# Graph attention and a DiT block on one core: self features of six more tiles added by VectorE, and two boundaries and the end in another order

## The chip, the cores and the metric

The kernel runs on one core of one Trainium2 chip. Its engines work side by side, each through its own queue in order: TensorE (PE; its weight loads are shown as PEld), VectorE (DVE), ScalarE (ACT), GpSimd (POOL), and SyncE (SP), which here only issues DMAs. The metric is the device time of one execution in microseconds, the median of several runs. An engine that waits for another waits on a semaphore, and whatever stands behind the waiting instruction in the same queue waits too.

## What is computed

Input x is 64 sequences of 64 tokens of 256 features. First a graph attention with a residual, then a transformer block whose norms are modulated by a condition:

```python
# graph attention, two directions d, 16 heads, 20 keys per sequence
self_feat = concat(v, q) @ W_self.T + b_self
output = self_feat
for d in range(2):
    aff = einsum('bnhd,bmhd->bnhm', qh, kh) / sqrt(dh)
    aff = where(cond > 0, aff, NEG) + (A_d @ w_bias + b_bias)
    out_t = einsum('bnhm,bmf->bnhf', softmax(aff), kv)
    output = output + einsum('bnhf,hgf->bnhg', out_t, Wout) + bout
x = v + relu(output)
# block: shift, scale, gate from silu(cond) @ Wt + bt
h = layernorm(x) * (1 + scale_msa) + shift_msa
x = x + gate_msa * (attention(h) @ Wproj + bproj)
h = layernorm(x) * (1 + scale_mlp) + shift_mlp
x = x + gate_mlp * (gelu(h @ W1 + b1) @ W2 + b2)
```

All of it is float32.

## The kernel before, in words

The 64 sequences are cut into nine groups of 4, 8, 8, 8, 8, 8, 8, 8 and 4 (numbers 0 to 8); two sequences make a tile of 128 tokens, so a group has 4 tiles, the outer ones 2. Features lie on partitions (`xT`, `sfT`, `hT`: 128 partitions, 2 halves c, tokens). The residual stream of a group stays in `xT`, is added to in place, and is stored from there.

The order is written out by hand: each function records its instructions on the engines it uses, and the order of the calls is the order in every queue. `start` does group 0's graph part, `boundary(g)` stands between the periods, `period(g)` runs the tiles of a group, `finish` ends. A `slot` takes one tile e of block attention and one tile c of the next group's graph attention: scores of both (L755, L756), then the softmax parts, with the transposes, attention products and outputs of the slot before (Eb, Cb), and other work put in by name (`fill("f1")` and so on). While group g is in block attention, group g+1 is in graph attention, g−1 in its MLP, and g+2 has its self features and masks made. The parts that matter:

- `graph_turned` (L490): eight transposes of the weights to PSUM (pwT), two ScalarE copies to wT. `graph_output` (L502): 16 small products of wT with `vblk` into po. For groups 0 to 2 (`early`, L507) two products with the identity first put self features into po, and ScalarE takes the relu straight from PSUM (L521). For the others VectorE adds po to sf (L523) and ScalarE takes the relu in SBUF (L524). POOL adds the result to xT (L525).
- `norm_tokens` (L528): four transposes of xT (pxT), a ScalarE copy xn; `norm_stats` (L537): five VectorE instructions and a power on POOL (L546); `normed` (L548): two VectorE instructions (L551); `modulated` (L556): four transposes (phT), a VectorE product (L563), a POOL sum (L567).
- `graph_exp` (L476): VectorE maxima and subtraction, ScalarE exp. `graph_normal` (L483): sum, reciprocal, POOL product (L488). `block_exp`, `block_sums`, `block_weights` (L624 to L643): the same for block attention, with a POOL product pr (L643).
- `mask_step(g, i)` (L338): seven VectorE steps for a group's masks and biases, 0 to 2 for one direction, 3 to 5 for the other, 6 for three last instructions.
- `graph_v` (L363): values, through DRAM (L374, L389) into vblk (L395). `graph_q` (L416): one of four q products (pqT), copied by ScalarE.
- `block_qk` (L573), `block_keys` (POOL, L597), `block_attended` (L659: pao, copied by ScalarE at L675). `block_proj` (L686): the projection of a whole group for one half c. `pair_proj` (L697): the same for two tiles and both halves.
- `mlp_up`, `mlp_down` (L717, L727), `mlp_gated`, `mlp_out` (L735, L743): the last ends with the store of a half.

PSUM has eight banks. Scores use two pairs ("pa", "pb"); `bank` (L89) hands out the other four in turn, and an accumulator of `mlp_down` holds its bank until `mlp_gated`:

```python
    def bank(name, hold=False):
        tag = free.pop(0)
        if not hold:
            free.append(tag)
        t = ps.tile([P, 512], F32, tag=tag, name=name)
        return (t, tag) if hold else t
```

A bank's new user waits for the last reader of its old contents.

In `boundary(g)` VectorE's order around the graph output is: values, mask steps (from 2 on at g = 1, all seven at g = 2, steps 4 to 6 later), then what follows graph_output.

Of the kernel before, what the change touches and what calls it, by code (L numbers as in the profile page):

```python
# [9 lines left out]
F32 = mybir.dt.float32  # L10
# [7 lines left out]
P = 128  # L18
# [28 lines left out]
def graph_attention_then_dit_block(  # L47
# [454 lines left out]
    def graph_output(t, po):  # L502
# [3 lines left out]
        po2 = po[:, 0:D].rearrange("p (c t) -> p c t", c=2)  # L506
        early = t.g < 3  # L507
        if early:
# [187 lines left out]

    def pair_proj(g, j2):  # L697

        G = groups[g]
        py = bank("pproj").rearrange("p (c t) -> p c t", c=2)  # L700
        t2 = ts(j2, 2 * P)
        for c in range(2):
            for k in range(2):
                nc.tensor.matmul(
                    py[:, c], wproj_sb[:, k, ts(c, P)], G.aoT[:, k, t2], start=(k == 0), stop=(k == 1)
                )
        y = two.tile([P, GT], F32, tag="tq", name="y").rearrange("p (c t) -> p c t", c=2)
# [6 lines left out]
        nc.gpsimd.tensor_tensor(G.xT[:, :, t2], G.xT[:, :, t2], y, ALU.add)  # L714

# [35 lines left out]
    def slot(e, c, e_next, c_next, before, fill, late=False):  # L751
# [29 lines left out]
        fill("d0b")  # L781
        if E:

            block_weights(E)
# [3 lines left out]
        for i, t in enumerate(Cb):  # L788
# [3 lines left out]
            graph_output(t, pair("pa" if i > 0 else "pb", "po")[:, 0])  # L792
        if C and late:
            graph_exp(C)
        fill("f2b")
        fill("d1")
# [6 lines left out]
    def boundary(g, before):  # L803
# [8 lines left out]
        if c_on:  # L812
            graph_v(g + 1, 1)
            for i in range((2, 0)[g - 1] if g < 3 else 4, 7):
                mask_step(g + 1, i)
        if m_on and c_on:
            mlp_out(g - 2, 1)
        block_turned(Eb)
        for t in Cb:
            graph_turned(t)  # L820
        if not c_on:
            mlp_down(g - 2, 1, *range(4))
        if c_on:
# [11 lines left out]
        if Cb:  # L835
            norm_tokens(G, G.xT, 1)
            norm_stats(G)
        block_proj(g - 1, 0)
        if Cb:
            normed(G)  # L840
        block_proj(g - 1, 1)
        if c_on:
            graph_q(g + 1, 1, 0)
        if Cb:
            modulated(G, G.hT, 1, amp1, off1, g)
        K = [Tile() for _ in range(A.nt // 2)]
        if not c_on:
            mlp_down(g - 2, 1, 4, 5)
        if c_on:
            graph_k(g + 1, 1)  # L850
        for j2, k in enumerate(K):
            norm_tokens(k, A.xT, j2)
            norm_stats(k)
# [16 lines left out]
        if e_on:  # L870
            block_qk(g, 0, 1)
        if c_on:
            graph_q(g + 1, 1, 1)
# [31 lines left out]
    def period(g):  # L905
# [35 lines left out]
        else:  # L941
# [38 lines left out]
    def start():  # L980
# [74 lines left out]
        for t in t1:  # L1055
# [27 lines left out]
                "f2a": [(self_product, 2, 1)],  # L1083
                "f3": [
                    (self_features, 2, 1), (mask_step, 2, 0), (block_v, 0, 0), (half_normed, 1, 0),
                    (mask_step, 2, 1), (time_projection, 3),
                ],
            },
# [4 lines left out]
                "f2b": [(time_product, 4), (time_product, 5), (time_sum, 4), (time_sum, 5)],  # L1093
                "f3": [(half_normed, 1, 3), (time_added, 4)],
            },
# [3 lines left out]
    def finish(before):  # L1099
# [83 lines left out]
        mlp_out(z, 0)  # L1183
        mlp_down(z, 1, *range(8))
        mlp_gated(z, 1)
        mlp_out(z, 1)

# [64 lines left out]
```

## Time and profile before

| what | value |
|---|---|
| median of 3 runs | 685.67 us (683.94 to 686.73) |
| profiled execution | 682.96 us |
| its span in the profile | 681.3 us |
| granted TensorE clock | 1.0 |
| idle before PE matmuls: start, 0 to 12 us | 2.3 us |
| 12 to 60 | 2.3 us |
| stretch 60 to 105 (end of start, boundary 1) | 4.5 us |
| 105 to 147 (period 1) | 2.0 us |
| 147 to 543, five periods with their boundaries | about 0.4 us |
| 543 to 578 (boundary 7) | 1.1 us |
| 604 to 653 (finish) | 2.9 us |
| 673 to 681.3 (end) | 4.2 us |

The profile is one execution on the hardware, and its times are in microseconds unless they are marked ns. A float32 matmul shows as two records, so counts of PE rows are twice the number of matmuls in the code. A timeline row has the start, the time, the engine, the line, the operation, the output and the inputs, the shapes and the count; in brackets stands how long the engine had been idle and what ended that. Rows of PE overlap, since matmuls are pipelined: the distance from one start to the next is what a row costs, not its length. A wait row has who waited, for whom, the total, how often, and the longest.

### The profile page before, as it was taken

What the parts mean: (1) busy time and instruction counts of PE and PEld (TensorE: products, weight loads), DVE (VectorE), ACT (ScalarE), POOL (GpSimd) and SP (SyncE); (2) the same over time, 40 slices, a digit from 0 to 9 for tenths busy, and PEclk for the clock granted to TensorE, in tenths of its full rate; (3) what the DMA queues carried; (4) which work ended last, traced back from release to release, by engine and by line L of the source; (5) the groups of instructions that cost most, each with busy time, mean ns of one, the idle gap of its engine ahead of it and who ended that gap; (6) DMA issues with size and microseconds to landing.
All of it is one profiled execution on the core that took longest, in us unless ns stands there. A gap on an engine that the chain in (4) does not pass through costs nothing.

```text
span 681.3 us, 15434 instructions
## 1 busy us (share of the span) xinstructions
PE 661.0 (97%) x6422; PEld 405.4 (60%) x6422; DVE 477.6 (70%) x849; ACT 354.6 (52%) x627; POOL 375.4 (55%) x371
## 2 busy tenths in 40 slices
PE   8999899999999999999999999999999999999997
PEld 7656657775555555556556555555565655556456
DVE  4988956797787677875876867776777865666221
ACT  3355437653576437654476435764377446754412
POOL 6555455755584476645584656744666456355220
PEclk9999999999999999999999999999999999999999
DMA  9535040004000220004000141002000000000000
GB/s 280 163 89 166 21 134 17 18 21 135 17 1 29 70 90 16 7 27 154 1 17 17 36 135 17 2 32 72 27 10 11 17 26 1 3 16 1 17 15 32
DMA packets 34382, 33.42 MB, mean 49 GB/s; under 512 B 5608, under 2 KB 28200, under 8 KB 34312
## 3 DMA queue, kind: packets, MB, share of 16 engines
q1 hardware_dynamic: 33352, 31.74, 15.1%
q8 instruction: 51, 0.84, 0.5%
q0 software_dynamic: 272, 0.33, 0.3%
q10 hardware_dynamic: 688, 0.35, 0.2%
q14 instruction: 19, 0.16, 0.1%
HBM read 25.59 MB, written 6.83 MB: 48 GB/s over the span
## 4 chain that ended last, share of the span: by engine, by line
PE 78%; DVE 13%; ACT 3%; POOL 2%; issue 2%; DMA 1%; SPq 0%; ACTq 0%; POOLq 0%; DVEq 0%
PE pu L723 14%; PE py L733 13%; PE pqT L422 8%; PE pqk L580 7%; PE ppT L654 4%; PE pv L588 3%; PE pf L324 3%; PE pwT L496 3%; PE pproj L690 3%; PE po L514 2%; PE pv L371 2%; PE pk L407 2%; PE phT L560 2%; PE pao L665 2%; PE sca L618 2%
## 5 line engine op out<-in xcount | busy, mean ns | idle before, releaser
L733 PE MATMUL py<-u,w 128*128 128x512 f32 (+1 forms) x288 | 121.4, 551 | 0.2 <-ACT u L725 0.2
L723 PE MATMUL pu<-h2T,w 128*128 128x512 f32 (+1 forms) x256 | 108.8, 570 | 0.5 <-POOL h2T L567 0.5
L643 POOL TENSOR_TENSOR pr<-pr,sm 128x1024 f32<-128x1024 f32 x32 | 60.8, 1901 | 66.9 <-DVE sm L642 64.0
L474 POOL TENSOR_TENSOR w<-w,term 128x640 f32<-128x640 f32 x32 | 49.4, 1547 | 77.8 <-DVE w L469 40.3
L723 PEld LDWEIGHTS pu<-h2T,w 128*128 128x128 f32 x256 | 47.9, 190 | 48.6 <-issue 42.7
L733 PEld LDWEIGHTS py<-u,w 128*128 128x128 f32 x288 | 50.8, 190 | 36.4 <-issue 33.0
L725 ACT ACTIVATE u<-pu,vec 128x512 f32<-128x512 f32 (+1 forms) x72 | 43.3, 639 | 35.5 <-PE pu L723 35.2
L422 PE MATMUL pqT<-sfT,wq 128*128 128x512 f32 (+1 forms) x144 | 60.9, 551 | 0.7 <-DVE a L350 0.7
L580 PE MATMUL pqk<-hT,wqkv 128*128 128x512 f32 (+1 forms) x144 | 59.7, 552 | 0.6 <-POOL hT L567 0.4
L629 DVE TENSOR_REDUCE mx<-sca 128x8 f32<-128x512 f32 x32 | 22.1, 691 | 51.8 <-PE sca L458 50.3
L551 DVE TENSOR_SCALAR xn<-xn,mv,rstd 128x256 f32<-128x256 f32 x64 | 50.1, 823 | 7.7 <-POOL rstd L546 7.7
L639 DVE TENSOR_REDUCE sm<-pr 128x16 f32<-128x1024 f32 x32 | 38.9, 1217 | 21.4 <-ACT pr L635 20.7
L481 ACT ACTIVATE w<-w 128x640 f32<-128x640 f32 x32 | 23.6, 736 | 54.4 <-DVE w L480 54.4
L542 DVE BATCH_NORM_STATS2 st<-xn 128x6 f32<-128x256 f32 x64 | 26.1, 408 | 34.7 <-ACT xn L535 34.7
L488 POOL TENSOR_TENSOR w<-w,sm 128x640 f32<-128x640 f32 x32 | 44.0, 1376 | 11.7 <-DVE sm L487 11.5
L423 ACT ACTIVATE qT<-pqT,vec 128x512 f32<-128x512 f32 (+1 forms) x36 | 23.0, 639 | 52.6 <-PE pqT L422 52.5
L635 ACT ACTIVATE pr<-pr 128x1024 f32<-128x1024 f32 x32 | 33.8, 1057 | 30.1 <-DVE pr L631 29.9
L546 POOL TENSOR_TENSOR rstd<-rstd,mhalf 128x2 f32<-128x2 f32 x32 | 23.3, 728 | 46.7 <-DVE rstd L545 45.9
L657 ACT COPY pT<-ppT 128x512 f32<-128x512 f32 x64 | 34.4, 590 | 26.4 <-PE ppT L654 26.4
L581 ACT ACTIVATE qk<-pqk,vec 128x512 f32<-128x512 f32 (+1 forms) x36 | 23.0, 640 | 43.3 <-PE pqk L580 43.3
L500 ACT COPY wT<-pwT 80x512 f32<-80x512 f32 x64 | 34.0, 581 | 13.9 <-PE pwT L496 13.9
L525 POOL TENSOR_TENSOR xT<-xT,sfT 128x256 f32<-128x256 f32 x32 | 24.1, 753 | 28.6 <-ACT sfT L524 16.3
(144 smaller groups left out, 1424.6 us busy)
## 6 DMA issues: line engine op xcount, KB each, us to landing
xT<-in_x_t SPq DMA_DIRECT2D x7, 512.0 KB
out<-xT SPq DMA_DIRECT2D x14, 256.0 KB
a_d<-in_adj SPq DMA_DIRECT2D x7, 440.0 KB
a_d<-in_adj_t SPq DMA_DIRECT2D x7, 440.0 KB
x_g<-in_x SPq DMA_DIRECT2D x5, 512.0 KB
vblk<-vd SPq DMA_DIRECT2D x28, 80.0 KB
w<-in_w SPq DMA_DIRECT2D x2, 1024.0 KB
vd<-v_sb SPq DMA_DIRECT2D x7, 256.0 KB
```

The source lines that it names most:

```text
L422: nc.tensor.matmul(pq, wq_sb[d][:, k, ts(c, P)], G.sfT[:, k, :], start=(k == 0), stop=(k == 1))
L474: nc.gpsimd.tensor_tensor(t.w, t.w, G.term[:, :, j, :].unsqueeze(1).to_broadcast([P, H, 2, M]), ALU.add)
L488: nc.gpsimd.tensor_tensor(wf, wf, sm.unsqueeze(2).to_broadcast([P, 2 * H, M]), ALU.mult)
L500: nc.scalar.copy(t.wT[:, ts(q4, 4), :], pt[0 : 4 * M, :].rearrange("p (i t) -> p i t", i=4))
L551: nc.vector.tensor_scalar(key.xn[:, i, :], key.xn[:, i, :], key.mv[:, i, 0:1], key.rstd[:, i : i + 1], ALU.subtract, ALU.mult,)
L580: nc.tensor.matmul(pp, wqkv_sb[:, k, ds(i * D + c * P, P)], G.hT[:, k, 0 : G.T], start=(k == 0), stop=(k == 1))
L639: nc.vector.tensor_reduce(t.sm, t.pr, AX.X, ALU.add)
L643: nc.gpsimd.tensor_tensor(t.pr, t.pr, t.sm.unsqueeze(2).to_broadcast([P, H, N]), ALU.mult)
L657: nc.scalar.copy(t.pT[:, ts(q4, 4), :], pt.rearrange("p (i t) -> p i t", i=4))
L723: nc.tensor.matmul(pu, w1_sb[:, k, ts(m, P)], G.h2T[:, k, 0 : G.T], start=(k == 0), stop=(k == 1))
L725: nc.scalar.activation(G.u[m], pu, AF.Gelu, bias=col("b1", m))
L733: nc.tensor.matmul(G.py, w2_sb[:, m, ts(c, P)], G.u[m], start=(m == 0), stop=(m == 7))
```

## The change

It has seven edits.

1. `early` holds for group 0 and the first two tiles of group 1 only, so for tiles (1,2), (1,3) and (2,0) to (2,3) the two identity products go, and VectorE adds self features.
2. In a slot marked late, `block_weights` is recorded after the graph output and `graph_exp`. In the first slot of the start, `self_features(2, 1)` comes at d1, and mask step 1 of group 2 leaves for boundary 1.
3. In boundary 1 the mask steps are 3, 1, 2, 4 ahead of the transposes and 5, 6 behind the graph output, followed by `time_added(4)`, which was in the start. `graph_q(2, 0, 0)` moves ahead of the second transposes, and `graph_q(2, 1, 1)` from the end of the boundary to behind `graph_q(2, 1, 0)`.
4. In the periods, the third step of `half_normed` (`normed`) is recorded at d0b, ahead of `block_weights`, and no longer at d1.
5. Boundary 7 has an order of its own, with the projection by pairs of tiles, the two q products earlier and the second pair's transposes between qk products.
6. In period 7 a down product moves behind attention. In the finish one pao takes a bank of the four instead of a pair; v and the scores of z's second tile come behind two down products and a norm; a down product comes ahead of the last transposes but one.
7. The last half of the last group is computed, gated, added and stored in two parts of 128 tokens.

```diff
-        early = t.g < 3
+        early = t.g == 0 or (t.g == 1 and j < 2)
...
-        if E:
+        if E and not late:
             block_weights(E)
...
-        if C and late:
+        if late:
             graph_exp(C)
+            block_weights(E)
...
-            for i in range((2, 0)[g - 1] if g < 3 else 4, 7):
+            for i in (3, 1, 2, 4) if g == 1 else range(0 if g == 2 else 4, 7):
                 mask_step(g + 1, i)
...
         block_turned(Eb)
+        if g == 1:
+            graph_q(2, 0, 0)
         for t in Cb:
             graph_turned(t)
...
+        if g == 1:
+            mask_step(2, 5)
+            mask_step(2, 6)
+            time_added(4)
...
+        if g == NG - 2:
+            pair_proj(g - 1, 0)
             norm_tokens(G, G.xT, 1)
             norm_stats(G)
             normed(G)
+            pair_product(g - 1, 1)
             graph_q(g + 1, 1, 0)
+            norm_tokens(K[0], A.xT, 0)
+            pair_gated(g - 1, 1)
             modulated(G, G.hT, 1, amp1, off1, g)
+            pair_added(g - 1, 1)
+            graph_q(g + 1, 1, 1)
+            graph_k(g + 1, 1)
+            norm_stats(K[0])
...
             block_qk(g, 1, 0)
+            if g == NG - 2:
+                norm_tokens(K[1], A.xT, 1)
+                norm_stats(K[1])
             block_qk(g, 1, 1)
...
-        if c_on:
+        if c_on and g not in (1, NG - 2):
             graph_q(g + 1, 1, 1)
...
-                    "d1": next_(half_normed, 2),
+                    "d0b": next_(half_normed, 2),
...
+            fills[1].update(f0=down(0, 0), f2=down(0, 1))
...
-        block_attended(before[0], pair("pa", "pao")[:, 0])
+        block_attended(before[0], bank("pao"))
...
-        block_v(z, 0)
         block_normal(E0)
-        E1 = block_scores(z, 1, [pair("pa", "sca"), pair("pb", "scb")])
-        mlp_down(l, 1, 4)
+        mlp_down(l, 1, 4, 5)
         norm_tokens(K[1], A.xT, 1)
         norm_stats(K[1])
-        mlp_down(l, 1, 5, 6)
+        block_v(z, 0)
+        E1 = block_scores(z, 1, [pair("pa", "sca"), pair("pb", "scb")])
         normed(K[1])
         block_turned(E0)
+        mlp_down(l, 1, 6)
...
+        mlp_down(m, 0, 0)
         block_turned(E1)
-        mlp_down(m, 0, 0)
...
-        mlp_down(z, 1, *range(8))
-        mlp_gated(z, 1)
-        mlp_out(z, 1)
+        py, y = bank("py"), two.tile([P, GT], F32, tag="tq", name="y")
+        for j in range(2):
+            t = ts(j, P)
+            for i in range(8):
+                nc.tensor.matmul(py[:, t], w2_sb[:, i, P : 2 * P], Z.u[i][:, t], start=(i == 0), stop=(i == 7))
+            nc.vector.scalar_tensor_tensor(
+                y[:, t].rearrange("p (b n) -> p b n", n=N), py[:, t].rearrange("p (b n) -> p b n", n=N), col("b2", 1),
+                gate[:, 3, ds(Z.b0 + 2 * j, 2)].unsqueeze(2).to_broadcast([P, 2, N]), ALU.add, ALU.mult,
+            )
+            nc.vector.tensor_tensor(Z.xT[:, 1, t], Z.xT[:, 1, t], y[:, t], ALU.add)
+            nc.sync.dma_start(out[P : 2 * P, ds(Z.t0 + j * P, P)], Z.xT[:, 1, t])
```

`pair_product`, `pair_gated` and `pair_added` are `pair_proj` cut in three: its products, its two VectorE instructions, and POOL's add.

More of the change, by code (lines that the diff above doesn't have):

```diff
@@ L695, in block_proj, with pair_product @@
         nc.gpsimd.tensor_tensor(G.xT[:, c, :], G.xT[:, c, :], G.yT[c], ALU.add)
-    def pair_proj(g, j2):
+    def pair_product(g, j2):
         G = groups[g]
-        py = bank("pproj").rearrange("p (c t) -> p c t", c=2)
-        t2 = ts(j2, 2 * P)
+        py = G.pair = bank("pproj").rearrange("p (c t) -> p c t", c=2)
         for c in range(2):
@@ L704, in pair_proj, with pair_gated @@
                 nc.tensor.matmul(
-                    py[:, c], wproj_sb[:, k, ts(c, P)], G.aoT[:, k, t2], start=(k == 0), stop=(k == 1)
+                    py[:, c], wproj_sb[:, k, ts(c, P)], G.aoT[:, k, ts(j2, 2 * P)], start=(k == 0), stop=(k == 1)
                 )
-        y = two.tile([P, GT], F32, tag="tq", name="y").rearrange("p (c t) -> p c t", c=2)
+    def pair_gated(g, j2):
+        G = groups[g]
+        py = G.pair
+        y = G.yp = two.tile([P, GT], F32, tag="tq", name="y").rearrange("p (c t) -> p c t", c=2)
         b4 = ds(G.b0 + 4 * j2, 4)
@@ L713, in pair_proj, with pair_added @@
             )
-        nc.gpsimd.tensor_tensor(G.xT[:, :, t2], G.xT[:, :, t2], y, ALU.add)
+    def pair_added(g, j2):
+        G = groups[g]
+        t2 = ts(j2, 2 * P)
+        nc.gpsimd.tensor_tensor(G.xT[:, :, t2], G.xT[:, :, t2], G.yp, ALU.add)
+    def pair_proj(g, j2):
+        pair_product(g, j2)
+        pair_gated(g, j2)
+        pair_added(g, j2)
     def mlp_up(g, m):
@@ L822, in boundary @@
             mlp_down(g - 2, 1, *range(4))
-        if c_on:
+        if c_on and g > 1:
             graph_q(g + 1, 0, 0)
@@ L834, in boundary @@
             load_adj(g + 2)
-        if Cb:
+        K = [Tile() for _ in range(A.nt // 2)]
+        if g == NG - 2:
+            pair_proj(g - 1, 0)
             norm_tokens(G, G.xT, 1)
             norm_stats(G)
-        block_proj(g - 1, 0)
-        if Cb:
             normed(G)
-        block_proj(g - 1, 1)
-        if c_on:
+            pair_product(g - 1, 1)
             graph_q(g + 1, 1, 0)
-        if Cb:
+            norm_tokens(K[0], A.xT, 0)
+            pair_gated(g - 1, 1)
             modulated(G, G.hT, 1, amp1, off1, g)
[L846 to L849, printed above, removed]
+            pair_added(g - 1, 1)
+            graph_q(g + 1, 1, 1)
             graph_k(g + 1, 1)
-        for j2, k in enumerate(K):
-            norm_tokens(k, A.xT, j2)
-            norm_stats(k)
+            norm_stats(K[0])
+        else:
+            if Cb:
+                norm_tokens(G, G.xT, 1)
+                norm_stats(G)
+            block_proj(g - 1, 0)
+            if Cb:
+                normed(G)
+            block_proj(g - 1, 1)
+            if c_on:
+                graph_q(g + 1, 1, 0)
+            if g == 1:
+                graph_q(2, 1, 1)
+            if Cb:
+                modulated(G, G.hT, 1, amp1, off1, g)
+            if not c_on:
+                mlp_down(g - 2, 1, 4, 5)
+            if c_on:
+                graph_k(g + 1, 1)
+            for j2, k in enumerate(K):
+                norm_tokens(k, A.xT, j2)
+                norm_stats(k)
         if c_on:
@@ L871, in boundary @@
             block_qk(g, 0, 1)
-        if c_on:
+        if c_on and g not in (1, NG - 2):
             graph_q(g + 1, 1, 1)
@@ L1083, in start @@
                 "f2a": [(self_product, 2, 1)],
[L1084 to L1087, printed above, removed]
+                "d1": [(self_features, 2, 1)],
+                "f3": [(mask_step, 2, 0), (block_v, 0, 0), (half_normed, 1, 0), (time_projection, 3)],
             },
@@ L1093, in start @@
                 "f2b": [(time_product, 4), (time_product, 5), (time_sum, 4), (time_sum, 5)],
-                "f3": [(half_normed, 1, 3), (time_added, 4)],
+                "f3": [(half_normed, 1, 3)],
             },
```

## The prediction, made before the run

> **What bounds the kernel now.** I read the page first, then the windows by stage, the PE waits, and the timelines of the stages that the change touches.
>
> ```profile
> PE 661.0 (97%) x6422; PEld 405.4 (60%) x6422; DVE 477.6 (70%) x849; ACT 354.6 (52%) x627; POOL 375.4 (55%) x371
> ```
> TensorE is busy for 661.0 of 681.3 us at a granted clock of 1.0. Only two things shorten this kernel: less TensorE work, or less of its 20 us of idle time. Where the idle time sits:
>
> ```profile
> 60.00:105.00 45.00, 40.47 (x465) 27.03 (x463) 33.49 (x62) 18.72 (x37) 21.90 (x24) 1.00 0.19 60
> 227.33:306.67 79.34, 79.28 (x775) 45.53 (x774) 59.01 (x104) 43.53 (x74) 47.18 (x45) 1.00 0.15 44
> ```
> Columns: stretch, length, then PE, PEld, DVE, ACT and POOL busy. A period of the middle has 0.06 us of idle PE, so no order can help there. The stretch with boundary 1 has 4.5 us, 105 to 147 has 2.0, 543 to 578 has 1.1 and 604 to 653 has 2.9. By cause (total, times, longest):
>
> ```profile
> PE phT L560 <- DVE xn L551: 2.6, 4, 1.5
> PE pao L665 <- DVE w L469: 1.8, 1, 1.8
> PE pwT L496 <- POOL w L488: 1.3, 2, 0.8
> PE pwT L496 <- DVE v_sb L387: 0.8, 1, 0.8
> PE pao L665 <- DVE pr L631: 0.7, 1, 0.7
> ```
> These are what the reordering can reach. The matmuls that it removes:
>
> ```profile
> 118.84 0.65 PE L665 MATMUL pao<-pT,v 128*32 128x64 f32 x32
> 119.42 0.71 PE L510 MATMUL po<-sfT,ident 128*128 128x128 f32 x4
> 120.06 0.74 PE L514 MATMUL po<-wT,vblk 80*32 80x64 f32 x32
> 120.73 1.98 PE L324 MATMUL pf<-xT,w_self 128*128 128x512 f32 x4
> ...
> 192.62 0.65 PE L665 MATMUL pao<-pT,v 128*32 128x64 f32 x32
> 193.10 0.80 PE L514 MATMUL po<-wT,vblk 80*32 80x64 f32 x32
> 193.83 1.99 PE L324 MATMUL pf<-xT,w_self 128*128 128x512 f32 x4
> ```
> From attention to the next product it is 1.89 us with the identity products and 1.21 without: 0.68 us a tile. Next to v's product (129.93 to 132.96 against 206.43 to 209.01) it is 0.45.
>
> **The change, part by part.** All sums are against the profiled execution.
>
> *Six adds to VectorE.* PE loses three times 0.65 and three times about 0.5: 3.4 us. VectorE gains six adds of 0.39 us (row of L523, 22 calls, 0.36 to 0.43): 2.4 us, with ScalarE's relu now behind them.
>
> *Start, 58 to 75.* VectorE takes the softmax subtraction before the reciprocal; it ran for 2.02 us beside POOL's 1.90 us product and should take its usual 0.83. One mask step (1.08) leaves. VectorE is then free when the scores end (65.4), so the maxima start at 65.5 rather than 66.32 and attention's wait falls from 1.75 to about 0.95: 0.8 gained. POOL now adds both tiles before its product, which waits for the second relu (61.6) and ends at about 64.3; the transposes that need it come at 65.6, so 1.3 us cover it. At 73.9 phT still meets VectorE, so this tile's identity saving is not seen yet.
>
> *Boundary 1, 75 to 104.* v_sb now stands ahead of amp/off (0.37 + 1.35 + 1.01), and a q product (1.72) comes ahead of the second transposes: the waits 0.52 and 0.76 vanish, and 0.64 of identity goes. At the end of L514 PE is 3.3 us ahead (81.2 for 84.5). The new add stands behind four mask steps (4.3 us from 77.5): 81.9 to 82.3, then relu 0.4 and POOL's add 0.75 give pxT at 83.65 where PE is there at 82.9: a new wait of 0.75. Stats are behind two more mask steps and amp/off, but two q products cover them (phT 89.25, before 90.83). The later waits for hT and xn (0.15 and 0.6) stay about as they are. The last q product no longer hides ScalarE's copy of the last qk (0.69): half of the scores wait 0.45. Graph scores at 101.0 instead of 104.37: 3.3 us gained in all, identity included.
>
> *Period 1, 105 to 147.* Slots 1 and 2 give 0.68 and 0.45; VectorE has 0.8 and 1.26 us to spare there, which its adds use up. In the last slot xn (2.27 us beside POOL) moves ahead of the reciprocal and takes 0.73; phT ends its wait 1.5 us earlier, but POOL's products start 0.7 later on that chain and w reaches pwT late: about 1.0 of it is left.
>
> *Boundary 2.* Here the add hurts.
> ```profile
> 148.91 0.29 DVE L387 TENSOR_TENSOR v_sb<-pv,bout 128x128 f32<-128x128 f32 x1 [0.72 <-PE pv L382]
> 149.12 1.06 DVE L347 TENSOR_REDUCE cnt<-a_d 128x80 f32<-128x880 int32 x1
> ...
> 156.05 0.38 DVE L360 SCALAR_TENSOR_TENSOR term<-vb,bb,term 128x160 f32<-128x160 f32 x1
> ```
> VectorE's queue holds the seven mask steps without a gap, 7.3 us, and the add for tile 3 is recorded behind them. Before, ScalarE did the relu straight from PSUM at 154.43 and pxT ran at 156.11 unhindered. On the new clock v_sb is at 146.35, the masks end at 153.95, add, relu and POOL's add take 1.6: pxT at 155.6, while PE would be there at 153.2. 2.4 us of new idle time, with proj, q and everything of PE queued behind it. The lead at this pxT: 156.1 − 155.6 = 0.5 on top of 3.3, so 3.8.
>
> *Periods 2 to 6.* normed moves ahead of the reciprocal. PE has no wait there to lose; the reciprocal comes 0.7 later, and POOL's product would end at about 305.05 for a transpose at 308.26. Nothing, covered by 3 us.
>
> *Boundary 7.* Projection by pairs costs PE the same (1.73 + 1.73 for 3.44). It removes pxT's waits (0.5 each), but brings four: phT on xn (0.7), qk on hT (0.55), phT of the first pair, whose normed now stands on VectorE behind the second pair's stats, which need POOL's 1.27 us add, a transpose and a copy (1.0 to 1.5), and the uncovered last copy (0.4). Graph scores at 567.9 for 566.95: 0.95 lost; between 0.5 gained and 1.8 lost.
>
> *Period 7.* One down product goes behind attention; the wait 0.45 at 584.23 is set by ScalarE (copy, table load 1.28, exp 1.06, then wT), so it stays: nothing.
>
> *Finish.* pao moves from the pair to a bank and the 0.70 wait goes. But the bank is the one that the next held accumulator takes, and its reader stands late on ScalarE:
> ```profile
> 608.23 1.06 ACT L635 ACTIVATE pr<-pr 128x1024 f32<-128x1024 f32 x1
> 609.19 0.61 ACT L675 ACTIVATE aoT<-pao,vec 128x128 f32<-128x128 f32 x2
> ```
> PE idles from 606.9 to 609.85, and scores E0 come 1.0 late. The two down products put behind the projection, and v later, absorb that: at 630 it is 0.2 late. The down product ahead of the last transposes covers their 0.61: 0.6 gained net.
>
> *Last store.* Sixteen 256-column matmuls become thirty-two of 128. [...] The trace disagrees: eight transposes with 128x128 loads follow each other every 0.116 us (187.29 to 188.22), 256-column ones every 0.215, so 3.71 for 3.44: 0.27 lost. I take the trace. After PE, gate and add over 128 columns: 0.48 + 0.42 become about 0.35 + 0.29 (from the 512- and 256-column rows): 0.26 gained. The store: 3.0 us from issue (678.26) to the span's end; no row has 64 KB to HBM. [...] Sum: 0.2 gained, between 0.2 and 0.4; by the loads rule 1.3 lost.
>
> Sum: 3.8 − 0.95 + 0 + 0.6 + 0.2 = 3.65 us. The profiled execution took 682.96 (span 681.3 and 1.66 around it): 679.3. The runs' median is 685.67, 2.7 above; I take the same difference: **682.0**.
>
> **The rivals.** *All covers hold*: VectorE finishes the masks before boundary 2's po, or pairs cost nothing at boundary 7. Then 2.4 of the new wait and 0.95 come back: 3.65 + 2.0 + 0.95 = 6.6, 679.1. For it: the middle's boundaries have this very chain without a wait (312.35 to 314.79), with three mask steps. Against: boundary 2 has all seven.
> *The waits only change place*: PE loses 3.4 of work and each edit's gain meets the next late engine, above all in boundary 1, where VectorE has no gap of 1 us between 77 and 89. Then 3.4 less 2.4 (boundary 2), less 0.95, plus half of the rest (1.3): 1.3 gained, 684.4. This is also the case in which the order does not do what it is meant to.
> *Slower: VectorE's queue is the bound from 64 to 160.* Place: boundary 1's add and the stats behind it. If amp/off run at their contended 1.35 and 1.01, and the mask steps at 1.1 push stats past 89, phT waits to 93 and boundary 1's 3.3 turns into 0.5 lost; the slots give nothing, boundary 2's pxT is 2.0 late, boundary 7 loses 0.95, the finish and the store give 0.8: 2.6 lost, 688.3. It decides from an add of tile (1,3) that starts after about 84 on the old clock, against my 81.9. Against it: amp/off leave POOL's busy stretch (77.5 to 80).
>
> **How the numbers follow.** Forecast 0.42, all covers 0.27, waits change place 0.23, slower 0.08. 0.5% (3.4 us) is about what a measurement of this kernel tells from no change. The forecast lies just past it, some 0.6 of its cases beyond: faster 0.27 + 0.25 = 0.52, same 0.17 + 0.23 = 0.40, slower 0.08. Range: from the all-covers case with the end's best (678.7) to the misplaced waits with boundary 7's worst (685.2).
>
> **What would show it.** In the profile after: L510 x16 instead of x40 and PE busy near 658; L523 x28; no pwT wait on v_sb; a pxT wait on POOL's L525 of about 2.4 us near 153 (right: my boundary 2; absent: the first rival) and one below 1 us near 83 (larger: the slower case); a phT wait on xn above 1 us near 560; a py wait on aoT or its bank near 607; the last 32 matmuls in 3.7 us. If phT still waits 1.5 us at the end of period 1, the order of normed was not the cause. The prediction is wrong if boundary 1 gains under 2 us.

## The result, and the profile after

The changed kernel takes 684.39 us (median of 14 runs, 681.49 to 687.03), the kernel before 684.5 (median of 14 runs, 683.39 to 686.73). The ratio is 0.9993 with a 95% interval of 0.9976 to 1.001: no change. The forecast was 682.0 with a range from 678.7 to 685.2, so the time lies in the range, near its upper end, and the likeliest class, faster, did not come. The forecast had started from 685.67, a median of three runs; fourteen give 684.5.

The profiled execution took 687.03 us (span 685.3, granted clock 0.993), the slowest run of this kernel, and the profile of before had 682.96 (681.3, 1.0). Its page has for TensorE and the rest:

```profile
PE 662.1 (97%) x6422; PEld 407.6 (59%) x6422; DVE 468.2 (68%) x859; ACT 354.6 (52%) x627; POOL 371.8 (54%) x371
```

TensorE's busy time has risen by 1.1 us though products for 3.4 us are gone, because in two places the same products ran at half the clock (0.50, in the windows below). VectorE has more instructions and less busy time. To see where time went I use the start of every first product that writes graph scores into `scb` as an anchor: there are 30 in each trace, at the same places of the program. All values are us; the forecast column is the sum of the prediction's own steps.

| stretch, by anchors of before | before | after | difference | forecast |
|---|---|---|---|---|
| 0 to 65.24: start | 65.24 | 69.13 | +3.89 | 0 |
| 65.24 to 104.70: its end, boundary 1 | 39.46 | 36.51 | −2.95 | −3.3 |
| 104.70 to 135.83: three slots of period 1 | 31.13 | 32.22 | +1.09 | −0.5 with the next |
| 135.83 to 175.05: last slot, boundary 2 | 39.22 | 39.28 | +0.06 | see above |
| 175.05 to 492.40: periods 2 to 6 | 317.35 | 316.34 | −1.01 | 0 |
| 492.40 to 567.27: boundary 7 | 74.87 | 75.81 | +0.94 | +0.95 |
| 567.27 to the end: period 7, finish, store | 114.03 | 116.01 | +1.98 | −0.8 |
| span | 681.3 | 685.3 | +4.0 | −3.65 |

The first row is not the change's: no instruction ahead of 57 us has moved. The list of TensorE's waits (total, times, longest) begins so:

```profile
PE pk L407 <- POOL kv L332: 2.7, 2, 2.2
PE py L745 <- ACT aoT L675: 2.5, 1, 2.5
PE phT L560 <- DVE xn L551: 1.9, 4, 0.9
PE pxT L533 <- POOL xT L525: 1.7, 1, 1.7
PE pu L735 <- ACT v L595: 1.3, 1, 1.3
```

Of these the first is the start's, where the profile of before waits for 0.8 in all. The second is the finish's, the fourth boundary 2's; the fifth, in period 1, was in no forecast. Behind the first wait, the windows of the start show the clock (third number from the end):

```profile
10.20:11.90 1.70, 0.78 (x4) 0.63 (x4) 1.39 (x4) 0.00 (x0) 0.89 (x3) 0.78 1.08 381
11.90:13.60 1.70, 1.70 (x10) 1.70 (x9) 1.63 (x4) 0.42 (x2) 1.35 (x1) 0.50 1.05 384
13.60:15.30 1.70, 1.70 (x8) 1.61 (x8) 1.60 (x5) 0.54 (x3) 0.00 (x0) 0.50 1.07 372
15.30:17.00 1.70, 1.70 (x6) 1.34 (x5) 1.52 (x2) 0.46 (x2) 1.49 (x2) 0.50 1.10 351
```

After TensorE had stood for 2.19 us it had half its clock (0.50) for 6.82 us, from 11.15 to 17.97. The start with the old instructions can have that too: an experiment below that has them (`pao_bank_only`) reaches its anchor at 67.14 instead of 65.24, with a clock of 0.50 at 14 us. This fits the changed kernel's times, which follow their granted clock: 681.49, 681.67 and 682.52 at 0.999, and 685.83 to 687.03 at 0.992 or 0.993. Stages are therefore compared by the anchors, and a dip of the clock is named where it lies in a stage.

In the finish the first attention product has its bank, and TensorE's rows are (in brackets the idle time ahead):

```profile
607.65 0.65 PE L665 MATMUL pao<-pT,v 128*32 128x64 f32 x32
608.24 0.66 PE L560 MATMUL phT<-ident,xn 128*128 128x128 f32 x4
608.73 0.60 PE L533 MATMUL pxT<-ident,xT 128*128 128x128 f32 x4
611.87 3.67 PE L745 MATMUL py<-u,w 128*128 128x512 f32 x4 [2.54 <-ACT aoT L675]
615.38 1.89 PE L580 MATMUL pqk<-hT,wqkv 128*128 128x256 f32 x8
```

The wait of 0.70 ahead of pao is gone, one of 2.54 stands behind it, and then four products take 3.51 us until the next one starts, where the same four need 2.01 without the stall (605.42 to 607.43 in the first experiment). The windows say why:

```profile
608.48:611.89 3.41, 0.87 (x9) 0.63 (x7) 2.21 (x4) 2.93 (x5) 2.27 (x2) 1.00 0.05 18
611.89:615.30 3.41, 3.41 (x4) 1.49 (x5) 2.91 (x7) 0.40 (x1) 2.18 (x2) 0.50 0.16 64
```

TensorE has 0.87 us of work in the first and a granted clock of 0.50 in the second. So the finish lost 1.84 by the stall (2.54 less the 0.70) and 1.50 by the clock. Between the qk products at 615.38 and the gelu products at 641.69 the edits gain 1.72 back (26.31 us, before 28.03).

### The profile page after: what moved, and what is told of

Same layout as the page of the kernel before. It is cut to its first block, busy times and chain, and to the rows that moved or that the text cites. A ratio compares the mean times of both kernels' runs of the same rounds, so it can differ in the third digit from the quotient of the medians.

```text
span 685.3 us, 15453 instructions
## 1 busy us (share of the span) xinstructions
PE 662.1 (97%) x6422; PEld 407.6 (59%) x6422; DVE 468.2 (68%) x859; ACT 354.6 (52%) x627; POOL 371.8 (54%) x371
## 4 chain that ended last, share of the span: by engine, by line
PE 82%; DVE 8%; DMA 3%; ACT 3%; POOL 2%; issue 1%; ACTq 0%; DVEq 0%; SPq 0%; POOLq 0%
PE py L745 15%; PE pu L735 15%; PE pqT L422 8%; PE pqk L580 7%; PE pv L588 4%; PE ppT L654 4%; PE pwT L496 3%; PE pk L407 3%; PE pproj L690 3%; PE pf L324 3%; PE po L514 2%; PE pv L371 2%; PE pao L665 2%; PE sca L618 2%; PE phT L560 2%; PE pxT L533 2%
## 5 line engine op out<-in xcount | busy, mean ns | idle before, releaser
L745 PE MATMUL py<-u,w 128*128 128x512 f32 (+1 forms) x272 | 119.8, 568 | 2.7 <-ACT aoT L675 2.5
L745 PEld LDWEIGHTS py<-u,w 128*128 128x128 f32 x272 | 48.3, 192 | 39.3 <-issue 33.0
L422 PE MATMUL pqT<-sfT,wq 128*128 128x512 f32 (+1 forms) x144 | 62.4, 565 | 0.3 <-DVE y L713 0.3
L551 DVE TENSOR_SCALAR xn<-xn,mv,rstd 128x256 f32<-128x256 f32 x64 | 36.4, 609 | 8.3 <-POOL rstd L546 8.3
```

The costliest lines, as they stand in the source:

```text
L422: nc.tensor.matmul(pq, wq_sb[d][:, k, ts(c, P)], G.sfT[:, k, :], start=(k == 0), stop=(k == 1))
L551: nc.vector.tensor_scalar(key.xn[:, i, :], key.xn[:, i, :], key.mv[:, i, 0:1], key.rstd[:, i : i + 1], ALU.subtract, ALU.mult,)
L745: nc.tensor.matmul(G.py, w2_sb[:, m, ts(c, P)], G.u[m], start=(m == 0), stop=(m == 7))
```

## The experiments

The theory: the change gains about 4 us (boundary 1 mostly by its order, periods 2 to 6 by the earlier norm), and three of its own edits give it back: the bank in the finish with the clock behind it, the add behind seven mask steps in boundary 2, boundary 7's order; and a little is lost by the two parts of the last store, which share a PSUM bank. Rivals: waits only change place, so that nothing comes back when one edit is undone; or the VectorE adds themselves cost what the identity products gave. Each run was made beside runs of the kernel before on the same chip, and ratios are to these; the changed kernel's 0.9993 comes from other runs, so that differences of two ratios are good to some 0.2%, and the stages decide.

**The bank undone** (`pao_pair`)
```diff
-        block_attended(before[0], bank("pao"))
+        block_attended(before[0], pair("pa", "pao")[:, 0])
```


> The changed kernel with one edit undone: the first attention product of the finish goes to the pair of banks again and not to one of the four. Theory: the bank costs a TensorE stall of 2.54 us near 612 and, because TensorE stands for over 2 us, a granted clock of about 0.5 for 3.4 us after it. Undone, the stall and the dip of the clock go and a wait of about 0.7 us on pr comes back; from scores of the outer group (anchor 581.15 after) to the gelu products (pu at 641.69 after) the stretch is 1.5 to 2 us shorter, the whole 682.7. Rival 1, TensorE's work bounds the finish and the stall is absorbed by the products put behind it: the stretch stays within 0.4 us. Rival 2, the dip at 612 is the same accident as the one at 10 us and has nothing to do with the stall: some profile shows a dip near 612 here too.

680.29 us, ratio 0.9949 (0.9933 to 0.9966): 3.0 us less than the changed kernel by the ratios. From the last anchor to the end it takes 101.26 us instead of 104.15. Its rows at the same place:

```profile
603.91 0.66 PE L665 MATMUL pao<-pT,v 128*32 128x64 f32 x32 [0.70 <-DVE pr L631]
604.49 0.66 PE L560 MATMUL phT<-ident,xn 128*128 128x128 f32 x4
604.99 0.60 PE L533 MATMUL pxT<-ident,xT 128*128 128x128 f32 x4
605.42 1.88 PE L745 MATMUL py<-u,w 128*128 128x512 f32 x4
607.43 2.00 PE L580 MATMUL pqk<-hT,wqkv 128*128 128x256 f32 x8
```

The old wait of 0.70 is back, the stall is not there, and the clock is 1.0 up to the last product. TensorE's busy time is 658.1 us, as the prediction had it. The effect is larger than expected (3.0 for 1.5 to 2): stall and clock both count.

**The bank alone, in the kernel before** (`pao_bank_only`): the same line, the other way round.

> The kernel before with one word of the sixth edit: the finish's first attention product goes to a bank of the four. Theory: TensorE stands for 2.5 to 3 us near 607 until ScalarE has copied it out (a wait of py on aoT), and in a part of the runs the granted clock falls to about 0.5 for 3.4 us behind that. With the removed pao wait of 0.7 set against it 1.2 to 2.0 us lost without the dip and 1.7 more with it: 686 to 687 median. Rival, the products behind absorb it as I forecast (0.2 late at 630): 684.0.

687.53 us, ratio 1.003 (1.0016 to 1.0044). From the last anchor to the end 105.06 us instead of 102.17. The stall and the dip are those of the changed kernel:

```profile
612.46 2.94 PE L733 MATMUL py<-u,w 128*128 128x512 f32 x4 [2.54 <-ACT aoT L675]
```
```profile
611.00:612.70 1.70, 0.24 (x1) 0.24 (x2) 0.78 (x1) 1.70 (x4) 1.47 (x2) 1.00 0.20 78
612.70:614.40 1.70, 1.70 (x4) 0.64 (x4) 1.60 (x6) 0.18 (x1) 0.80 (x1) 0.69 0.20 76
614.40:616.10 1.70, 1.70 (x5) 0.99 (x4) 1.09 (x2) 0.00 (x0) 1.60 (x2) 0.50 0.00 0
```

So this one word costs 2.9 us in either surroundings where the clock falls too. Of 22 runs those with a clock of 0.999 or more took 684.87 to 685.82, which is 1.3 to 2.2 above the lowest of before (683.61); ten runs at 0.994 and 0.995 took 688.39 to 689.18.

**Boundary 2 with its mask steps split** (`masks_behind_b2`)
```diff
-            for i in (3, 1, 2, 4) if g == 1 else range(0 if g == 2 else 4, 7):
+            for i in (3, 1, 2, 4) if g == 1 else range(0, 3) if g == 2 else range(4, 7):
...
+        if g == 2:
+            for i in range(3, 7):
+                mask_step(3, i)
```


> The changed kernel with the seven mask steps of boundary 2 split as boundary 1 has them: steps 0 to 2 ahead of the graph output, 3 to 6 behind it. The add of self features stays on VectorE. Theory: the add costs something only because seven steps are queued ahead of it; with three ahead the pxT wait of 1.7 us on POOL near 157 goes, at most 0.5 of later waits (stats behind four steps) comes in its place, and the anchor at 177.14 comes 1.2 to 1.7 us earlier against the one at 137.86: the whole 682.9. Rival, the chain through VectorE, ScalarE and POOL is long in itself (add, relu, add: 1.6 us where there was a relu and an add): the wait stays above 1 us, or the stats behind the masks hold phT for as long, and nothing is gained (684.4).

682.43 us, ratio 0.9971 (0.9961 to 0.9981), 1.5 us less by the ratios; but from the anchor of period 1's last slot to the one behind boundary 2 only 0.56 less (38.72 us for 39.28). First VectorE in the changed kernel, then the transposes of both:

```profile
154.82 1.07 DVE L352 TENSOR_REDUCE vb<-a_d 128x80 f32<-128x880 f32 x1
...
156.36 0.39 DVE L360 SCALAR_TENSOR_TENSOR term<-vb,bb,term 128x160 f32<-128x160 f32 x1
156.66 0.42 DVE L523 TENSOR_TENSOR sfT<-po,sfT 128x256 f32<-128x256 f32 x1
```
```profile
156.28 0.38 PE L533 MATMUL pxT<-ident,xT 128*128 128x128 f32 x2
158.38 0.44 PE L533 MATMUL pxT<-ident,xT 128*128 128x128 f32 x2 [1.72 <-POOL xT L525]
```
```profile
152.37 0.60 PE L533 MATMUL pxT<-ident,xT 128*128 128x128 f32 x4
...
158.83 0.78 PE L560 MATMUL phT<-ident,xn 128*128 128x128 f32 x4 [0.71 <-DVE xn L551]
161.07 0.98 PE L533 MATMUL pxT<-ident,xT 128*128 128x128 f32 x7 [0.26 <-POOL xT L695]
```

The place in VectorE's queue makes the wait, as the theory says: with three steps ahead it is gone. But the statistics are now behind four steps, and 0.97 us of new waits come in its place. The rival has the larger half. What the ratio shows beyond the 0.56 is probably the start's clock, which was full in this profile, while the finish's dip is in it too.

**Boundary 7 as before** (`b7_as_before`): the branch for `g == NG - 2` and its two other places taken out, so that the general order holds.

> The changed kernel with boundary 7 in its old order (projection by halves, norms of both pairs together, the last q product at the end). Theory: the order of its own costs 0.94 us by four new waits; old, the stretch from the anchor at 493.48 to the one at 569.29 is 0.9 us shorter (74.9 us for 75.8), the pxT waits of about 0.5 us come back and are in that already; the whole 683.5. Rival, the loss was carried into the boundary by the end of period 6 and not made by the order: no difference (684.4).

682.35 us, ratio 0.998 (0.9969 to 0.9991). The stretch takes 74.61 us instead of 75.81: 1.20 less, since the earlier norm gives 0.26 here too. Its stall in the finish is the same 2.54 us, but the window behind it has a clock of 1.00:

```profile
607.27:610.68 3.41, 1.98 (x5) 1.02 (x6) 2.41 (x6) 1.86 (x4) 2.27 (x3) 1.00 0.20 77
610.68:614.10 3.42, 3.42 (x20) 2.69 (x19) 2.37 (x4) 1.24 (x3) 3.32 (x5) 1.00 0.00 0
```

So such a stall lowers the clock in some executions only (the last section has the numbers); from the last anchor to the end it is 102.52 us here, 1.26 more than with the pair, against 2.89 with the dip.

**All of it mended** (`all_mended`): the three edits above and, at the end, two banks:
```diff
-        py, y = bank("py"), two.tile([P, GT], F32, tag="tq", name="y")
+        pys, y = [bank("py"), bank("py")], two.tile([P, GT], F32, tag="tq", name="y")
...
-            t = ts(j, P)
+            t, py = ts(j, P), pys[j]
```


> The changed kernel with all four at once: pair for the finish's first attention product, mask steps 3 to 6 of boundary 2 behind the output, boundary 7 in its old order, and the two parts of the last half in two PSUM banks instead of one. Theory: the losses add up, 1.7 + 1.4 + 0.9 + 0.25 = 4.2 us, for 680.2 at the clock of the usual runs and about 678 at a full clock. Rival, the waits change place (what is gained at boundary 2 waits again at boundary 3 or in the finish): 682.5 to 684. Rival, the kernel is bound by TensorE's work and the clock decides all: 684.

677.63 us, ratio 0.9905 (0.989 to 0.992): 6.0 us less than the changed kernel by the ratios, more than the theory had, at a clock of 0.999 to 1.0 in all four runs. By the stages 5.4 us of it lie where the edits are (finish and store 3.7, boundary 7 1.2, boundary 2 0.5), and 0.7 in period 1's slots, which none of them touches. Both rivals fall for the whole: what each part gives back adds up.

**The last store in one piece** (`mended_old_store`): the mended kernel with the old last three calls.

> The mended kernel with the last half of the last group in one piece, as before: sixteen products, one gate, one add, one store. Theory: two parts in two banks are worth 0 to 0.3 us, since 32 loads with 128 columns cost 0.27 us more on TensorE and the gate, the add and the store after it get shorter by 0.26 and up to 0.15: 677.6 to 677.9 (677.63 with two parts). [...] Rival 2, the store's own time goes with its size: one piece is 0.5 or more slower, 678.2.

678.45 us, ratio 0.9911 (0.9889 to 0.9933), not told apart by the time (677.52 to 678.08 at full clock). The end tells it: from the last products that wait for gelu to the end of the span it takes 8.15 us (669.74 to 677.89) in one piece, as before (8.16), 7.76 in two parts with two banks (667.92 to 675.68), and 8.48 in the changed kernel, where the second part waits for the gate that reads the first out of the same bank:

```profile
679.38 0.35 DVE L1227 SCALAR_TENSOR_TENSOR y<-py,vec,gate 128x128 f32<-128x128 f32 x1 [0.77 <-PE py L1226]
679.76 0.29 DVE L1231 TENSOR_TENSOR xT<-xT,y 128x128 f32<-128x128 f32 x1
679.78 1.86 PEld L1226 LDWEIGHTS py<-u,w 128*128 128x128 f32 x16 [0.64 <-DVE y L1227]
679.78 2.05 PE L1226 MATMUL py<-u,w 128*128 128x128 f32 x16 [0.45 <-DVE y L1227]
```
In the mended kernel there is no such gap:
```profile
668.45 3.73 PE L1211 MATMUL py<-u,w 128*128 128x128 f32 x32
```

**The adds alone, in the kernel before** (`adds_only`)
```diff
-        early = t.g < 3
+        early = t.g == 0 or (t.g == 1 and j < 2)
```


> The kernel before with the first edit alone: six tiles get their self features by a VectorE add, all orders as before. Theory: the identity products are worth 3.4 us of TensorE only where VectorE has room. In boundary 1 the add falls behind four mask steps and amp and off and its gain is mostly eaten (anchor 65.24 to 104.70: 39.46 us before, 36.5 with all edits; here about 38.8); the slots of periods 1 gain about 0.5 each; boundary 2 loses its 1.7 us pxT wait. In all within 0.7 us of before: 683.5. Rival 1, the adds give all they promise: 3.4 us, 680.4, and boundary 1 alone shows 1.2 us. Rival 2, the adds bring boundary 1's whole 2.9 us (then the order there did nothing): 681.5 or less.

690.47 us, ratio 1.0084 (1.0058 to 1.011): slower, which no theory had; the profiled execution was the fastest of its six runs. Boundary 1's stretch takes 40.04 us, 0.58 more than with the identity products, the next 31.18 (+0.05), and the last slot with boundary 2 43.43 for 39.22. There the add is behind the seven mask steps without any lead in TensorE's queue to give away:

```profile
159.45 0.44 PE L533 MATMUL pxT<-ident,xT 128*128 128x128 f32 x2 [2.40 <-POOL xT L525]
159.72 5.29 PE L690 MATMUL pproj<-aoT,wproj 128*128 128x512 f32 x8
```
```profile
156.86:160.27 3.41, 1.01 (x6) 0.58 (x5) 1.22 (x5) 1.34 (x3) 0.72 (x1) 1.00 0.86 249
160.27:163.69 3.42, 3.42 (x6) 1.36 (x5) 2.12 (x7) 0.24 (x1) 0.72 (x2) 0.50 1.06 363
```

A wait of 2.40 us, the clock at half behind it (the projection takes 5.29 us for its usual 3.6), and ahead of it, in the last slot, a wait of phT on xn of 1.96 for 1.5. VectorE's queue as the bound, which the prediction priced as its slower rival for the changed kernel, is what the adds are without the new orders.

**The earlier norm alone, in the kernel before** (`normed_only`)
```diff
-                    "d1": next_(half_normed, 2),
+                    "d0b": next_(half_normed, 2),
```


> The kernel before with the fourth edit alone: the norm's last step is recorded ahead of the reciprocal in the last slot of each period. Theory: it removes a wait of 0.26 us in each of periods 2 to 6 that the list of TensorE's waits hides (from phT to the next product 0.71 us before, 0.44 after), and in period 1 most of the 1.5 us wait of phT on xn. Periods 79.08 us for 79.34, so 1.3 over five, and 0.5 to 1.0 in period 1: 681.7. Rival, as I forecast: nothing in periods 2 to 6, and 1.0 in period 1: 682.8. Rival 2, the gain of 0.26 in the changed kernel came from its other edits, and this one gives nothing: 683.8.

682.42 us, ratio 0.997 (0.9956 to 0.9984): faster by 2 us. The last slot of period 1 with boundary 2 takes 38.18 us for 39.22, periods 3 to 6 79.08 or 79.09 each for 79.34 (period 2 79.28). This line of the change is a gain by itself, and the theory holds. The wait in the periods shows in no list; it lies in the distance of two rows, first before, then after the change:

```profile
304.94 0.87 PE L560 MATMUL phT<-ident,xn 128*128 128x128 f32 x4
305.65 1.02 PE L733 MATMUL py<-u,w 128*128 128x512 f32 x2
```
```profile
306.80 0.60 PE L560 MATMUL phT<-ident,xn 128*128 128x128 f32 x4
307.23 1.02 PE L745 MATMUL py<-u,w 128*128 128x512 f32 x2
```

The four transposes take 0.71 us until the next product starts, and 0.43 with xn made earlier. They wait between each other, in the midst of one row's busy time: before, their starts lie 0.32, 0.17 and 0.11 us apart, after, 0.11 each.

**The orders without the adds** (`mended_no_adds`): the mended kernel with `early = t.g < 3`.

> The mended kernel with the first edit undone: all tiles of groups 0 to 2 get their self features by the identity products again, in the new orders. Theory: with the orders mended the adds are worth something, but less than their 3.4 us of products: boundary 1 loses 0.6 to 0.8 by them (its 2.9 us came mostly from the order), the slots of period 1 0.66, the last slot with boundary 2 about 0.5: 1.9 us in all, 679.5. Rival 1, the order did all of it and the adds nothing: 677.6 to 677.9. Rival 2, each identity product counts in full: 3.4 us, 681.0.

679.61 us, ratio 0.9931 (0.9919 to 0.9944), by the ratios 1.8 us more than with the adds, by the spans 2.1. The sum is the theory's, its terms are not: boundary 1 takes 36.84 us without and 36.52 with the adds, so that 2.6 of its 2.9 us come from the order and 0.3 from the adds. The three slots of period 1 lose 1.06 without them, but the last slot with boundary 2 takes 38.17 without and 38.75 with them: there the add costs 0.58 even with the masks split. Another 1.07 is lost in periods 2 to 6, 0.99 of it in period 2, where ScalarE's copies of the values start 3.21 us late. So the adds are worth 0.8 us here and not 3.4, and 0.6 of this is that in period 1, too, ScalarE's copies stand for 1.74 us without them and for 1.11 with them. That they stand less because of the adds is not shown; without this the adds give 0.2.

**A cover for period 1's new wait** (`mended_v_cover`)
```diff
-                    "f3": up(0, 1, 2, 3),
+                    "f3": up(0, 1, 2) + (up(3) if g > 1 else []),
...
-                    "f3": up(4, 5),
+                    "f3": ([] if g > 1 else up(3)) + up(4, 5),
```


> The mended kernel with three gelu products instead of four behind the values in the first slot of period 1, the fourth at the end of the second slot. TensorE stood 1.2 us there, for the bank that ScalarE's late copies of the values had yet to free. Theory: only the fourth product needs that bank, scores are ready to go and are behind it in the queue; moved, the wait of 1.2 us goes and the anchors behind it come 0.8 to 1.2 earlier: 676.6. Rival, ScalarE itself is late, and what follows (exp, the table load, the gelu copies) makes TensorE wait as long in the second slot: 677.6.

678.56 us, ratio 0.9923 (0.9907 to 0.9939): 0.9 us slower, which neither had. It is nearer to the rival: the scores go earlier, but the transposes behind them wait for 1.15 us on POOL's pr and 0.48 on ScalarE's gelu copies, and the moved product meets a new wait of 0.50 on VectorE. In the two slots TensorE waits for 2.60 us with the cover and for 1.83 without. What is late is ScalarE. Its rows in the changed kernel and in the one before:

```profile
109.37 1.48 ACT L595 COPY v<-pv 64x256 f32<-64x256 f32 x4
112.09 1.50 ACT L595 COPY v<-pv 64x256 f32<-64x256 f32 x4 [1.24 <-PE pu L735]
113.61 0.74 ACT L481 ACTIVATE w<-w 128x640 f32<-128x640 f32 x1
```
```profile
108.43 3.01 ACT L595 COPY v<-pv 64x256 f32<-64x256 f32 x8
111.72 0.74 ACT L481 ACTIVATE w<-w 128x640 f32<-128x640 f32 x1 [0.28 <-DVE w L480]
```

The last of the products that it copies had ended before 110 us, and still ScalarE stands. The profile of before has the same standing, 2.05 us, at 182.30, where products of 512 columns cover it (7.03 us of them from 178.99).

**Five adds** (`mended_less_one_add`): the mended kernel with identity products for tile (2,3) again, and the seven mask steps in one piece.

> The mended kernel with the add of one tile undone, (2,3), the one of boundary 2, whose mask steps then all stand ahead of the output again: five adds instead of six. Theory: at that boundary the add costs even with three mask steps ahead of it (anchor to anchor 38.75 us with it, 38.17 without any adds, 39.22 before), so without it 0.4 to 0.6 less: 677.1. Rival, the 0.58 us came from the other adds of that stretch (the last slot's) and the identity products of this tile cost their 0.65: 677.9 to 678.3.

676.89 us, ratio 0.9889 (0.9868 to 0.9909): 0.7 us less than with six by the spans (675.0 and 675.7), and the lowest median of all kernels here, though the intervals of the two overlap. The stretch is 38.17 us, as without any adds, for 38.75. So the whole cost at boundary 2 was this one tile's.

## Why the prediction held in part

*Busy time.* 3.4 us of identity products: near (661.0 to 658.1, where no stall slows the clock). What this is worth in time was wrong: the adds give 0.8 us net in the mended kernel, and alone they lose 6.

*Boundary 1.* 3.3 forecast, 2.95 measured, and with the forecast's reason: two q products moved, 2.6 by order and 0.3 by the adds. The pxT wait of 0.75 did not come; scores waited for 0.46 as said (0.45).

*Period 1 and boundary 2.* 0.5 gained was forecast, 1.15 lost. The last slot's gain (about 1.0) came: 1.04 with that edit alone. Boundary 2's new wait was read from the right rows and came out at 1.72 for 2.4: the transposes of the pair's first tile did not have to wait (0.38), and TensorE had stood for 0.46 on POOL's w on its way there. The step that failed is "Slots 1 and 2 give 0.68 and 0.45". By the anchors they gave −0.06 and 0.18. Between the mended kernel and the same without the adds, which differ by the adds alone, they give 0.11 and 0.32 (11.47 us for 11.58, 10.18 for 10.50). The rows of slot 1 before:

```profile
119.84 0.74 DVE L331 SCALAR_TENSOR_TENSOR sfT<-pf,vec,tq 128x512 f32<-128x512 f32 x1
```
And after:
```profile
121.73 0.74 DVE L331 SCALAR_TENSOR_TENSOR sfT<-pf,vec,tq 128x512 f32<-128x512 f32 x1
122.53 1.98 PE L324 MATMUL pf<-xT,w_self 128*128 128x512 f32 x4 [0.47 <-DVE sfT L331]
```

In both, the second self features product starts just behind VectorE's step on the first (before, that ends at 120.58 and the product starts at 120.73): the identity products filled time that TensorE now waits for. The nine profiles with the adds have this wait of 0.47, the four without them have none. "1.89 us with the identity products and 1.21 without" was the misreading: the 1.21 is from period 2, where that step ends 0.29 us ahead of the product. The slot before these two lost 1.21, since ScalarE stood for 1.24 us in front of its copies; it was not in the working. Why it stands is open: its products are done, and in all eight profiles of kernels with boundary 1's new order and the adds it stands for 1.0 to 1.5 us there. In the profile of before TensorE waits for nothing at this place, but for 0.5 to 0.8 us on these copies in the three with one edit alone, two of which have the same instructions up to here: the standing differs between executions of the same order.

*Periods 2 to 6.* "PE has no wait there to lose" was wrong by 1.0 us. I took 0.06 us of idle time in 79.34 for proof that no order could help; a wait between the transposes of one row counts as busy.

*Boundary 7.* +0.95 forecast, +0.94 measured, with three of the waits named: phT 0.38 (0.7 forecast), phT of the first pair 0.92 (1.0 to 1.5), qk copy 0.47 (0.4). The wait of qk on hT (0.55) did not come, and one of q on VectorE (0.33) was not forecast. That the sums agree is in part luck: the order alone costs 1.20, and the earlier norm gives 0.26 in this stretch.

*Finish.* This is the step that cost most. The stall was forecast (606.9 to 609.85, and it was 2.54 us); "The two down products put behind the projection, and v later, absorb that" was not so. TensorE is busy for 97%, and a product placed behind a stall does not shorten it; it can only take the place of a later wait, and there was 1.72 us of those. And half the clock behind a stall was in no term: 1.5 us more.

*Store.* 0.2 gained was forecast for two parts, 0.3 lost: the parts share a bank, and the second waits 0.45 us for VectorE's read of the first. With two banks 0.4 is gained. The forecast's choice of the trace for the products was right: 32 products of 128 columns took 3.73 us, for 3.71 forecast. No run shows a ground for "by the loads rule 1.3 lost", nor for the term that the sum of 0.2 to 0.4 has for the store itself (up to 0.15 in the expectation of `mended_old_store`). Measured from the last issue to the span's end are 2.75 us for a store of 64 KB (682.58 to 685.33) and 3.00 for one of 128 KB in the profile of before.

*The sum.* Span against span the miss is 7.65 us: 3.89 at the start, which is no part of the change, 0.35 in boundary 1, 1.65 in period 1 and boundary 2, 2.78 in the finish with the store, less 1.01 in the periods and 0.01 in boundary 7. Of the medians it is 2.4: the profile after lies 2.6 above its kernel's median and that of before 1.5 below, and 685.67, from which the forecast was taken, is 1.2 above the median of fourteen runs. This last is luck. As a change from before, the range says 0.5 to 7.0 us less and the forecast 3.65; measured is 0.1 less. No change, which had a chance of 0.40, came about through a gain in boundary 1 of the size that was forecast, one of 1.0 in the periods that was not, and losses: two of them named by the working (boundary 7, and the stall of the finish, taken for absorbed), the others, the clock, ScalarE's standing and the wait on self features, not. In the first rival 2.0 is added for boundary 2's wait of 2.4; with 2.4 it is 678.7, and nothing else changes.

## What to carry to other kernels

A bank that serves an early product costs what its reader's queue costs (a stall of 2.54 us in the finish here): look who takes that bank next, and when the engine that empties it comes to it. Moving work onto an engine is worth its price only with the queue in front of it mended: the same six adds lost 6 us in the old order and gave 0.8 at most in the new. A product taken away saves little where the next one waits for another engine anyway: 0.11 us in slot 1 of period 1, with a wait of 0.47 on VectorE in its place. And where an edit packs several moves, take each alone; the best kernel here (676.89 us) is the change without its bank in the finish, without its order of boundary 7 and with one add fewer, and with a bank for each part of the last store.

## What was not expected of the hardware

A stall of TensorE of 2.2 to 2.5 us can halve its clock. In the changed kernel it is 0.50 from 11.15 to 17.97, 6.82 us, after 2.19 us at the start, and from 611.89 to 615.30, 3.41 us, after 2.54 in the finish; in `adds_only` it is 0.50 from 160.27 to 163.69, 3.42 us, after 2.40 in boundary 2. But the same 2.54 us left it at 1.00 in the profile of `b7_as_before`, and so did 1.72 us in boundary 2 of the changed kernel (1.00 from 154.50 to 161.33). So the length of the stall does not tell by itself whether it costs clock. Nor do the numbers on the work that TensorE had ahead: the 3.41 us ahead of the falls in the finish and in boundary 2 have 0.87 and 1.01 us of it, but 3.40 us with 1.09 in `b7_as_before` (606.40 to 609.80) have a clock of 1.00 behind them. At the start the clock is 0.50 from 13.60 to 15.30 in `pao_bank_only` and `mended_old_store` too, and the 3.40 us from 8.50 to 11.90 had 1.95 and 2.66 us of work there, at 1.00. Which of such stalls costs clock stays open here.

ScalarE stands for 0.73 us (`adds_only`, period 1) to 3.21 us (`mended_no_adds`, period 2) ahead of the second half of its copies of the values in one period or another, with its input ready and no engine in its way. An instruction load of 16 KB starts 3.30 us ahead of the first of those copies in the profile after (at 106.07) and takes 4.14 us, where most take about 1; in the profile before one takes 3.03 at the same place (105.07), and nothing stands. Whose instructions these loads carry is not shown, and the profile after has loads as slow (3.91 at 177.44, 4.07 at 256.29) with no stand behind them. Nothing here shows the cause, and no run tried it by itself.
